# Splitting h·W1[D:] into its leading and its low part in PSUM instead of on VectorE, with other places for the row and list pieces

## The chip, the core and the metric

The kernel runs on one core of a Trainium2 chip, with TensorE (PE, and PEld for its weight loads), VectorE (DVE), ScalarE (ACT), GpSimd (POOL) and the DMA queues. The metric is the time of one execution on the device, in microseconds (us).

## The reference, cut to what matters

There are B = 16 graphs over the same N = 1024 nodes with D = 256 features, and one sparse adjacency matrix (about 0.8% of the entries and the diagonal are not zero).

```python
pre_u = einsum('bud,dk->buk', h, W1[:d])
pre_v = einsum('bvd,dk->bvk', h, W1[d:])
hidden = relu(pre_u[:, :, None, :] + pre_v[:, None, :, :] + b1)
S   = sigmoid(einsum('buvk,ko->buvo', hidden, W2)[..., 0] + b2[0])
a_t = einsum('buv,bud->bvd', S * A_a, h)
m_t = einsum('uv,bud->bvd', A_m, h) * h
z_t = beta1 * h + beta2 * (a_t @ Wa + ba) + beta3 * (m_t @ Wm + bm)
```

The kernel works on the edges alone. A *block* is 4 of the 16 graphs and 128 of the 1024 target nodes v; there are 32 blocks. A block has two windows of 64 target nodes, and a window has five chunks of 128 edges, so that a block is ten *steps*, s = 0 to 9, and the kernel has 320 steps, n = 0 to 319.

## The kernel before

For each step, 128 rows of a table in DRAM are gathered by edge (`fetch`): a row holds pre_u of four graphs and then h of four graphs. Then, in this order:

```python
def expand(n):                      # PE: pre_v, one row an edge, two steps ahead
    pcs[n] = psc.tile([P, GD], FP, name="pc")
    for h in range(2):
        nc.tensor.matmul(pcs[n][:, c], marks[n // TW][:, j * P:(j + 1) * P], cuts[k][:, w, c], start=True, stop=True)

def left_adj(n):                    # ACT: the edge's weight at the target's place
    nc.scalar.activation(lefts[n][:, :m, :, 0, :], onehot[...], AF.Copy, scale=val[:, i, j:j + 1])

def gate(n):
    nc.vector.tensor_tensor(t, fetched[n % NF][:, :GD]..., pcs.pop(n)..., ALU.add)     # DVE, 128x1024
    for b in range(GB):
        nc.vector.scalar_tensor_tensor(t[:, b, :], t[:, b, :], 0.0, w2_b, ALU.max, ALU.mult, accum_out=sc[:, b:b + 1])
    nc.scalar.activation(gt, sc, AF.Sigmoid, bias=b2_b)                                # ACT
    for b in range(GB):
        nc.scalar.activation(lefts[n][:, :m, b, 1, :], lefts[n][:, :m, b, 0, :], AF.Copy, scale=gt[:, b:b + 1])

def aggregate(n):                   # PE, a step later: sums over edges into acc
    for b in range(GB):
        nc.tensor.matmul(accs[h]..., left[:, i, b]..., f[:, GD + b * D:GD + (b + 1) * D], ...)
```

`expand` multiplies by a matrix of zeros and ones in float32r. To lose nothing, pre_v + b1 of a block is split into a leading part, rounded to float32r, and a low part. `X` holds both: for window 0 the leading parts of its 64 nodes lie in partitions 0 to 63 and the low parts in 64 to 127, and for window 1 the other way round. `halves` makes X for the next block, in two halves of 512 columns:

```python
def halves(k):
    X = cuts[k] = big.tile([P, NW, GD], FR, name="X")
    low = one.tile([P, GD], FR, name="low")
    for h in range(2):
        step = yield
        c = slice(2 * h * D, (2 * h + 2) * D)
        p = small("p")
        add_row(p, b1_p)                                  # PE: the bias
        half_product(p, hTs[order[k]], w_v, h, True)      # PE: h W1[D:]
        nc.scalar.copy(X[:, 0, c], p)                     # ACT: rounds to float32r
        after(step + 1, lambda c=c, p=p: nc.vector.tensor_tensor(
            low[:, c], p, X[:, 0, c].bitcast(FP), ALU.subtract))
    yield
    nc.scalar.copy(X[W:, 1, :], X[W:, 0, :].bitcast(FP))
    for w in range(NW):
        yield
        nc.scalar.copy(X[(1 - w) * W:(2 - w) * W, w, :], low[w * W:(w + 1) * W].bitcast(FP))
```

All tiles made by `small` are 128x512 of PSUM with the name "misc", and there are two buffers for them, taken in turn. The others that use them:

```python
def rows(k, tab=None):        # a row piece of the table: pre_u of 128 nodes, in two halves
    for h in range(2):
        step = yield
        p = small("p")
        half_product(p, hTs[k], w_u, h, False)
        nc.scalar.copy(tab[:, c], p)
    after(step + 1, lambda: nc.sync.dma_start(table[g][nt * P:(nt + 1) * P, :GD], tab))

def turn_over(k, w, q, step): # acc, copied out, is transposed into LT
    pt = small("pt")
    for i in range(4):
        nc.tensor.transpose(pt[:, i * P:(i + 1) * P], ev[:, r, c * P:(c + 1) * P], ident)
    nc.scalar.copy(LT..., pt...)
    # ... and after(step + 1): LT of A_m is multiplied by h on VectorE (times_h)

def block_end(k):             # LT times Wm and Wa, in four sends at s = 3, 4, 5, 6
    #   pz = small("pz") for each half; then after(step + 1):
    nc.vector.scalar_tensor_tensor(hb[:, 2 * h:2 * h + 2, :], hb[...], be1, pz..., ALU.mult, ALU.add)
```

`lists(vt)` makes the edge lists of 128 target nodes in about ten pieces, mostly small VectorE instructions; the lists of vt = 0 to 3 are made ahead of the steps and those of 4 to 7 among them. Each engine runs its instructions in the order in which the code emits them. The loop, cut:

```python
for n in range(total + 2):
    k, s = divmod(n, T)                       # T = 10
    aggregate(n - 1); fetch(n - 1 + NF)       # NF = 5 gather buffers
    # at s = 0, 3, 5, 8: acc is copied out (ACT, "ev")
    gate(n); left_adj(n + 1)
    if n % TW == 1: load_mark(n // TW + 1)    # ACT: a 128x640 cast, at s = 1 and 6
    do(n)                                     # what after() put here
    expand(n + 2)
    for i in advance.get(n, ()): next(made[i], None)           # list pieces
    # turn_over at s = 1 (of the block before), 7 (twice) and 9; block_end at 3 to 6
    if k + 1 < BS and s in (0, 2, 3, 4, 6): go(parts, n)       # halves of the next block
    if n in loads: load_hT(loads[n]); ...
    if n in at: go(piece, n)                                   # row pieces
```

## Time and profile before

The time is 1200.83 us, the median of three runs (1200.64 to 1201.29). The profiled execution has a span of 1195.2 us.

| group of the profile | count | mean of one | what it is |
|---|---|---|---|
| L539 DVE 128x1024 | 320 | 1215 ns | the addition of a gate |
| L543 DVE 128x256 | 1280 | 422 ns | relu, times W2, sum |
| L523 PE 128x512 | 640 | 454 ns | expand |
| L560 PE, 32 columns | 4096 records | 394 ns | aggregate, four at a time |
| L384 PE w_v and w_u | 448 records each | 384 and 390 ns | pre_v and the table rows |
| L608 PE | 992 records | 379 ns | LT times Wm and Wa |
| L612 DVE 128x512 | 62 | 744 ns | the sum into h_blk |
| L418 ACT 128x512 | 64 | 583 ns | the leading part into X |

A line of a group gives line, engine, operation, tiles (out<-in), shapes and count; then busy time in us, the mean of one in ns, and the idle time of the engine just before, with what ended it. A mean is a latency: instructions of one engine overlap at their ends, so that a series advances by less than the sum of the means. A float32 product stands as two records. A line of the time line gives start and length in us, then the same names, and in brackets the idle time of the engine before it.

### The profile page before, as it was taken

How to read it: one execution, taken by the hardware profiler on the slowest of the kernel's cores; microseconds unless marked ns; L12 is line 12 of the kernel's file. 1: busy time of each engine (PE TensorE's matmuls, PEld its weight loads, DVE VectorE, ACT ScalarE, POOL GpSimd, SP SyncE). 2: the span in 40 equal slices, each digit the busy share in tenths (PEclk: the TensorE clock that was granted, in tenths of full speed). 3: DMA queues.
4: the chain of work that ended last, by engine and by line, in shares of the span. 5: the costliest groups of instructions: out<-in, count | busy, mean ns of one | idle time of the engine just before them, and what ended most of it. 6: DMA issues, size and time to landing. Idle time of an engine off the chain costs nothing. (4 is left out here: it accounts for less than half of the span.)

```text
span 1195.2 us, 23788 instructions
## 1 busy us (share of the span) xinstructions
PE 1097.9 (92%) x7633; PEld 724.7 (61%) x7633; DVE 1066.9 (89%) x3515; ACT 840.4 (70%) x2498; POOL 426.1 (36%) x428
## 2 busy tenths in 40 slices
PE   7667988999889898999999999999999999999986
PEld 6544655666556565666666666666666666666653
DVE  8769879989988988899899999999999999999994
ACT  3346666677667665777777777787878777777873
POOL 1557652433263226333233333333333333333330
PEclk9968899999999999999999999999999999999998
DMA  9988889899979978999999999999999999999992
GB/s 279 312 307 261 258 319 333 315 336 377 320 254 373 361 244 302 357 384 360 351 329 379 359 331 371 362 356 386 358 367 345 356 324 326 326 341 328 335 340 76
DMA packets 147046, 391.39 MB, mean 327 GB/s; under 512 B 16752, under 2 KB 105328, under 8 KB 110704
## 3 DMA queue, kind: packets, MB, share of 16 engines
q0 software_dynamic: 50016, 300.50, 68.5%
q1 hardware_dynamic: 81616, 74.99, 19.6%
q10 hardware_dynamic: 15280, 14.29, 3.7%
q8 instruction: 63, 1.03, 0.3%
q14 instruction: 71, 0.58, 0.1%
HBM read 393.78 MB, written 50.33 MB: 372 GB/s over the span
## 5 line engine op out<-in xcount | busy, mean ns | idle before, releaser
L453 POOL DMA_INDIRECT fetched<-table,uidx x320 | 329.7, 1030 | 675.5 <-PE acc L560 509.6
L543 DVE SCALAR_TENSOR_TENSOR t<-t,w_b 128x256 f32<-128x256 f32 x1280 | 469.3, 422 | 20.1 <-ACT LT L581 0.5
L539 DVE TENSOR_TENSOR t<-fetched,pc 128x1024 f32<-128x1024 f32 x320 | 388.8, 1215 | 22.4 <-DMA fetched<-table,uidx 8.6
L560 PE MATMUL acc<-fetched,left 128*32 128x256 f32 x4096 | 334.2, 394 | 32.3 <-ACT left L549 16.8
L549 ACT ACTIVATE left<-left,gt 128x32 f32<-128x32 f32 (+1 forms) x1280 | 299.4, 304 | 10.4
L523 PE MATMUL pc<-X,mark 128*128 128x512 f32 x640 | 238.1, 454 | 21.1 <-DVE t L539 13.6
L560 PEld LDWEIGHTS acc<-fetched,left 128*32 128x32 f32 x4096 | 129.9, 110 | 177.2 <-issue 46.9
L546 ACT ACTIVATE gt<-sc,b_b 128x4 f32<-128x4 f32 x320 | 95.3, 298 | 140.5 <-DVE t L543 133.9
L523 PEld LDWEIGHTS pc<-X,mark 128*128 128x128 f32 x640 | 97.2, 191 | 156.6 <-issue 102.2
L608 PE MATMUL misc<-w_a,LT 128*128 128x256 f32 x496 | 127.3, 379 | 0.0
L608 PE MATMUL misc<-w_m,LT 128*128 128x256 f32 x496 | 127.1, 378 | 0.0
L384 PE MATMUL misc<-w_u,hT 128*128 128x256 f32 x448 | 109.2, 390 | 11.0 <-ACT few L298 3.6
L533 ACT ACTIVATE left<-onehot,val 128x128 f32<-128x128 bf16 (+1 forms) x320 | 116.5, 364 | 0.0
L384 PE MATMUL misc<-w_v,hT 128*128 128x256 f32 x448 | 107.9, 384 | 0.0
L543 DVE DVE_READ_ACCUMULATOR t<-t,w_b 128x1 f32 x1280 | 104.2, 81 | 0.0
L608 PEld LDWEIGHTS misc<-w_m,LT 128*128 128x128 f32 x496 | 93.7, 189 | 17.2
L384 PEld LDWEIGHTS misc<-w_u,hT 128*128 128x128 f32 x448 | 85.8, 195 | 27.3 <-issue 4.4
L608 PEld LDWEIGHTS misc<-w_a,LT 128*128 128x128 f32 x496 | 94.2, 190 | 12.8
L568 ACT COPY ev<-acc 128x512 f32<-128x512 f32 x128 | 75.1, 587 | 34.7 <-PE acc L560 26.8
L341 POOL DMA_INDIRECT val<-in_adjT_dram,vidx x80 | 83.6, 1046 | 33.4 <-issue 21.9
L384 PEld LDWEIGHTS misc<-w_v,hT 128*128 128x128 f32 x448 | 86.7, 194 | 14.3
L581 ACT COPY LT<-misc 128x512 f32<-128x512 f32 x128 | 71.1, 575 | 24.0 <-PE pc L523 12.0
(158 smaller groups left out, 830.9 us busy)
## 6 DMA issues: line engine op xcount, KB each, us to landing
h_blk<-in_x_dram SPq DMA_DIRECT2D x31, 512.0 KB
out_dram<-h_blk SPq DMA_DIRECT2D x31, 512.0 KB
hT<-in_xT_dram SPq DMA_DIRECT2D x28, 512.0 KB
table<-tab SPq DMA_DIRECT2D x26, 512.0 KB
table<-in_x_dram ACTq DMA_DIRECT2D x24, 512.0 KB
fetched<-table,uidx POOLq DMA_INDIRECT x320
table<-in_x_dram SPq DMA_DIRECT2D x8, 512.0 KB
table<-fetched SPq DMA_DIRECT2D x6, 512.0 KB
```

The source lines that it names most:

```text
L341: nc.gpsimd.indirect_dma_start(out=val[:, i, j:j + 1], out_offset=None, in_=adj_flat, in_offset=bass.IndirectOffsetOnAxis(ap=vidx[:, i, j: ...
L384: nc.tensor.matmul(p[:, bb * D:(bb + 1) * D], hT[:, 2 * h + bb, i, :], wt[:, i, :], start=(i == 0 and not begun), stop=(i == DC - 1), skip ...
L453: nc.gpsimd.indirect_dma_start(out=fetched[n % NF], out_offset=None, in_=table[g], in_offset=bass.IndirectOffsetOnAxis(ap=uidx[:, vt * NW ...
L523: nc.tensor.matmul(pcs[n][:, c], marks[n // TW][:, j * P:(j + 1) * P], cuts[k][:, w, c], start=True, stop=True)
L533: nc.scalar.activation(lefts[n][:, :m, :, 0, :], onehot[:, i, o:o + m, :].unsqueeze(2).to_broadcast([P, m, GB, V]), AF.Copy, scale=val[:, ...
L539: nc.vector.tensor_tensor(t, fetched[n % NF][:, :GD].rearrange("p (b d) -> p b d", b=GB), pcs.pop(n).rearrange("p (b d) -> p b d", b=GB), ...
L543: nc.vector.scalar_tensor_tensor(t[:, b, :], t[:, b, :], 0.0, w2_b, ALU.max, ALU.mult, accum_out=sc[:, b:b + 1])
L546: nc.scalar.activation(gt, sc, AF.Sigmoid, bias=b2_b)
L549: nc.scalar.activation(lefts[n][:, :m, b, 1, :], lefts[n][:, :m, b, 0, :], AF.Copy, scale=gt[:, b:b + 1])
L560: nc.tensor.matmul(accs[h][b * 2 * V:(b + 1) * 2 * V, r, :], left[:, i, b].rearrange("p k v -> p (k v)"), f[:, GD + b * D:GD + (b + 1) * D ...
L568: nc.scalar.copy(evs[q], accs.pop(q))
L608: nc.tensor.matmul(pz[:, bb * D:(bb + 1) * D], LTs[k][:, c, 2 * h + bb, i, :], wt[:, c, :], start=False, stop=(i == 1 and c == DC - 1), sk ...
```

## The change

The low part is no longer made by VectorE. TensorE adds minus one times the leading part to the PSUM tile that holds h W1[D:] + b1, so that the low part is what remains there, and ScalarE copies it from PSUM to its places in X. The copies are made half by half, right after that product, so `halves` needs two sends (s = 0 and 2) instead of five. The row pieces and list pieces get other places among the ten steps, some pieces ahead of the first step change their places too, and two pieces of list 3 move behind the first expansion.

```diff
+    minus = fixed([P, P], "minus", FR)
+    nc.vector.tensor_scalar(minus, ident, -1.0, None, ALU.mult)
 ...
     def halves(k):
         X = cuts[k] = big.tile([P, NW, GD], FR, name="X")
-        low = one.tile([P, GD], FR, name="low")
         for h in range(2):
 ...
             nc.scalar.copy(X[:, 0, c], p)
-            after(step + 1, lambda c=c, p=p: nc.vector.tensor_tensor(
-                low[:, c], p, X[:, 0, c].bitcast(FP), ALU.subtract))
-        yield
-        nc.scalar.copy(X[W:, 1, :], X[W:, 0, :].bitcast(FP))
-        for w in range(NW):
-            yield
-            nc.scalar.copy(X[(1 - w) * W:(2 - w) * W, w, :], low[w * W:(w + 1) * W].bitcast(FP))
+            def rest_of(c=c, p=p):
+                nc.tensor.matmul(p, minus, X[:, 0, c], start=False, stop=True, skip_group_check=True)
+                nc.scalar.copy(X[W:, 1, c], X[W:, 0, c].bitcast(FP))
+                for w in range(NW):
+                    nc.scalar.copy(X[(1 - w) * W:(2 - w) * W, w, c], p[w * W:(w + 1) * W])
+            after(step + 1, rest_of)
 ...
-    script = ("r 0 0", "r r 0", "r 1", "0 r 1 1", "0 0 r r", "1 r 0 2 2", "r r 0 0 v 2", "1 1 r r",
-              "2 r 1 r", "2 2 r r 1 1 h", "2 h 3 3", "2 2 h 3", "f h h 3", "3 3")
+    script = ("r 0 0", "r r 0", "r 1", "0 r 1 1", "0 r r 0", "1 r 0 2 2", "r r 0 0 v 2", "r r 1 1",
+              "2 1 r r", "2 r r 2 1 1 h", "2 h 3 3", "2 2 3", "f 3")
 ...
     for i, n in zip(range(EARLY, NT), (0, 20, 50, 80)):        # list pieces
-        for o in (0, 4, 5, 6, 7, 9, 11, 13, 15, 17):
+        for o in (0, 4, 6, 9, 11, 14, 16, 17, 19, 20):
 ...                                                            # (load, first half, second half) of the rows
-    plan(turn[NT:], ((0, 5, 8), (6, 12, 15), (12, 18, 22), (17, 25, 28), (24, 32, 35), (31, 38, 42), (38, 45, 48),
-                     (43, 50, 52)))
-    plan([(2, vt) for vt in range(NT)], ((62 + 10 * i, 68 + 10 * i, 73 + 10 * i) for i in range(NT)))
-    plan([(3, vt) for vt in range(NT)], ((146, 152, 157), (156, 162, 167), *((153 + 10 * i, 158 + 10 * i, 161 + 10 * i)
+    plan(turn[NT:], ((0, 7, 8), (3, 9, 11), (11, 18, 19), (15, 21, 28), (23, 29, 31), (32, 38, 39), (35, 41, 47),
+                     (42, 48, 49)))
+    plan([(2, vt) for vt in range(NT)], ((62 + 10 * i, 68 + 10 * i, 71 + 10 * i) for i in range(NT)))
+    plan([(3, vt) for vt in range(NT)], ((142, 148, 151), (152, 158, 161), *((153 + 10 * i, 158 + 10 * i, 161 + 10 * i)
                                                                              for i in range(2, NT))))
 ...
     left_adj(0)
+    for _ in range(2):
+        next(made[EARLY - 1])
 ...
-        if k + 1 < BS and s in (0, 2, 3, 4, 6):
+        if k + 1 < BS and s in (0, 2):
```

## The prediction

> **What bounds the kernel now.** I read the page's busy totals first, then the busy time by stretches, then the groups kept apart by shape, and last the time line of two blocks of ten steps. A block is found in the time line by the 128x1024 addition that opens each of its ten steps.
>
> The totals do not decide between two engines:
>
> ```profile
> PE 1097.9 (92%) x7633; PEld 724.7 (61%) x7633; DVE 1066.9 (89%) x3515; ACT 840.4 (70%) x2498; POOL 426.1 (36%) x428
> ```
>
> The stretches do. The columns are the window, its length, then busy time of PE, PEld, DVE, ACT and POOL, the clock, the DMA share and GB/s. The rows are blocks 0 to 10, 11 to 16, 18 to 23, 24 to 30, then block 21 alone and block 27 alone:
>
> ```profile
> 68.50:500.10 431.60, 387.33 (x2609) 256.15 (x2608) 379.96 (x1267) 289.42 (x860) 187.89 (x185) 0.95 0.89 311
> 500.10:700.80 200.70, 194.90 (x1371) 128.12 (x1372) 181.97 (x579) 152.98 (x460) 62.38 (x60) 0.99 0.97 359
> 733.10:927.70 194.60, 192.23 (x1389) 126.31 (x1388) 181.91 (x576) 153.26 (x462) 62.28 (x61) 1.00 0.99 361
> 927.70:1145.50 217.80, 209.73 (x1515) 133.14 (x1513) 210.83 (x672) 171.98 (x526) 71.55 (x71) 1.00 0.94 335
> 830.80:862.80 32.00, 31.43 (x229) 20.56 (x228) 30.31 (x97) 25.70 (x78) 9.72 (x10) 1.00 1.00 363
> 1021.10:1052.20 31.10, 29.96 (x218) 19.01 (x216) 30.12 (x96) 24.55 (x76) 10.20 (x11) 1.00 0.93 329
> ```
>
> Blocks 24 to 30 take 217.8 / 7 = 31.11 us each, and VectorE is busy 30.12 of block 27's 31.10: what is left is about 0.1 us between steps. They are bound by VectorE. Blocks 18 to 23, which also make table rows (two half products a block), take 32.4 on average and 32.0 at best, with both PE and VectorE near full. Blocks 0 to 10, with row pieces and lists, lose 431.6 - 380.0 = 51.6 us on VectorE.
>
> These groups carry the change (busy, then mean ns of one, then idle before):
>
> ```profile
> L419 DVE TENSOR_TENSOR low<-misc,X 128x512 fp32r<-128x512 f32 x64 | 43.9, 686 | 19.7 <-ACT X L418 19.7
> L425 ACT CAST X<-low 64x1024 fp32r<-64x1024 f32 x64 | 66.8, 1044 | 0.8
> L422 ACT CAST X<-X 64x1024 fp32r<-64x1024 f32 x32 | 33.4, 1042 | 0.4
> L581 ACT COPY LT<-misc 128x512 f32<-128x512 f32 x128 | 71.1, 575 | 24.0 <-PE pc L523 12.0 <-remote 4.8 <-PE misc L578 4.3
> ```
>
> And the places where they lie. Step 1 of block 27, ScalarE:
>
> ```profile
> 1026.75 0.30 ACT L546 ACTIVATE gt<-sc,b_b 128x4 f32<-128x4 f32 x1 [0.56 <-DVE t L543]
> 1027.08 0.96 ACT L549 ACTIVATE left<-left,gt 128x32 f32<-128x32 f32 x4
> 1027.94 0.39 ACT L533 ACTIVATE left<-onehot,val 128x128 f32<-128x128 bf16 x1
> 1028.23 0.71 ACT L516 CAST mark<-whose 128x640 fp32r<-128x640 uint8 x1
> 1028.84 0.58 ACT L581 COPY LT<-misc 128x512 f32<-128x512 f32 x1
> ```
>
> VectorE in the same block:
>
> ```profile
> 1026.63 0.69 DVE L419 TENSOR_TENSOR low<-misc,X 128x512 fp32r<-128x512 f32 x1
> 1027.23 1.21 DVE L539 TENSOR_TENSOR t<-fetched,pc 128x1024 f32<-128x1024 f32 x1
> ...
> 1029.86 0.69 DVE L591 TENSOR_TENSOR LT<-LT,hT 128x512 f32<-128x512 f32 x1
> ```
>
> Here LT, copied until 1029.42, is ready 0.44 us before VectorE multiplies it. In block 21, which makes rows, VectorE and then PE show:
>
> ```profile
> 836.32 0.68 DVE L419 TENSOR_TENSOR low<-misc,X 128x512 fp32r<-128x512 f32 x1
> ...
> 849.72 0.75 DVE L612 SCALAR_TENSOR_TENSOR h_blk<-h_blk,be,misc 128x512 f32<-128x512 f32 x1 [0.25 <-PE misc L608]
> ```
>
> ```profile
> 837.05 1.99 PE L384 MATMUL misc<-w_u,hT 128*128 128x256 f32 x8
> 838.98 1.07 PE L560 MATMUL acc<-fetched,left 128*32 128x256 f32 x16
> ```
>
> PE's row product starts at 837.05, just after the low subtraction ended at 837.00: the two PSUM buffers "misc" alternate, and the row product takes the one that held the v product. From there PE runs without a gap to the product that VectorE awaits at 849.72 (0.25 us idle), and VectorE runs without a gap to the next block's low. That is a closed loop of 31.98 us (gates at 830.78 and 862.76).
>
> **What the Trainium skill says.** "ScalarE: Activation LUTs", section "What ACT_TABLE_LOAD costs", gives 186 ns + 0.833 ns per element for an ACTIVATE with immediate operands, and an overlap of about 93 ns back to back. The trace agrees: 1,042 ns for 1,024 elements, 575 for 512, and a pair of LT copies covers 1.04 us, so the second adds about 0.47. "Perfetto Trace Analysis", section "Tensor Engine Instruction (MATMUL, LD_WEIGHTS)", says that ScalarE and VectorE are strict FIFOs; the time line shows ScalarE in program order throughout. The same page, "Optimization Strategy", says consistent bubbles can mean too few buffers; the wait of the row product on low is one. "TensorE: Matmul & The Clock Gate", "Wait — 56ns, not 53.3ns?", gives 215.7 ns start to start for 512 columns when warm; here the bias product to its follower is 1033.26 to 1033.49, 0.23, and a pc pair advances PE by 0.57.
>
> **The change, part by part.**
>
> 1. Removed from VectorE: two low subtractions a block. In block 27 a plain step is 2.81 us (1033.70 to 1036.51), and one with low 3.24 (1030.47 to 1033.70), so each is worth 0.43, not its 0.686 of latency. On VectorE alone the block would fall to 31.10 - 0.86 = 30.24.
>
> 2. Added to PE: two products with minus a block. By the pc pair each costs 0.57 / 2 = 0.28. Behind an X copy that is already done at 1026.19 and agg's end near 1026.1, it hardly waits.
>
> 3. Moved on ScalarE: three copies of 64x1024 in steps 3, 4 and 6 become six of 64x512, three in step 1 and three in step 3. The work grows by about 6 x 0.49 - 3 x 1.0, that is nothing; the place matters. In the program's order step 1 on ScalarE is now gate, left, next left, mark, three copies, LT copy. Three copies at 0.49 put the LT copy's end at 1029.42 + 1.46 = 1030.88. Without low VectorE is ready to multiply at 1029.86 - 0.43 = 1029.43. It waits 1.45, with the semaphore 1.5. Block 24 to 30: -0.43 (low in step 1) - 0.43 (in step 3) + 1.50 = +0.64 each, times 7 = +4.5 us. Later in the block nothing further is late: by step 3's copies ScalarE is some 0.2 us behind and recovers.
>
> 4. Row pieces go to steps 8 and 1 in all blocks of the middle (before, 8 and 3 up to block 16, 8 and 1 in blocks 18 to 23). In step 1 the row product takes the buffer of the v product, which is now freed by ScalarE's last copy of step 1, not by low. From gate to LT copy is 2.09 us in block 27; with three copies and the tail of the last, 2.09 + 1.46 + 0.09 = 3.6 after block 21's gate, which is at 836.43: 840.0 in place of 837.05, so PE starts 3.0 later. The rest of the loop is unchanged except for one minus product, +0.28. The loop becomes 31.98 + 3.0 + 0.28 = 35.3 us. Twelve blocks (11 to 16, 18 to 23) now take 200.7 + 194.6 = 395.3; at 35.3 they take 423.6: +28.3. Block 17, now 32.2, makes no rows in step 1: -0.4.
>
> 5. Blocks 0 to 10. The list pieces move off the steps with LT and h_blk work to 0, 4, 6, 9, and three waits of low on X (3.31, 4.42 and 2.02 us) vanish. Against that, step 1 row pieces in blocks 1 to 4 and 7 to 10 bring the loop of point 4, with the list's VectorE work inside it (about 3.6 us in a list's first block, 4.8 in its second). Block by block I get about 38 for 0, 40 for 1, 39 for 2, 40 for 3, 37 for 4, 38 for 5, 39 for 6, 35.5 for 7, 39 for 8, 40 for 9 and 35.6 for 10: 421 against 431.6, so -10. This is the softest term; the figures are estimates from the loop, the 12 us of one list's VectorE groups and the present block lengths.
>
> 6. Ahead of the first gate (68.5 us) one turn of the script goes and two list pieces move behind the first expansion: -2, an estimate.
>
> Sum: 1200.8 + 4.5 + 28.3 - 0.4 - 10 - 2 = 1221 us.
>
> **The rivals.** (a) VectorE is the bound and only its work counts: 31 blocks x 0.86 = 27 us less, about 1174. For it speaks VectorE's 97% in blocks 24 to 30; against it the order on ScalarE, where LT has only 0.44 us of slack and gets 1.46 us of copies ahead of it. (b) PE is the bound: 62 x 0.28 = 17 us more, 1218, or some 1210 with better places in the early blocks. Against it: PE in block 27 still has waits ahead of three acc groups (0.44, 0.22 and 0.48 us) that also stretch their records (1.21 for 0.64, 1.69 for 1.07 twice), some 2.9 us in all, so blocks without rows would not feel it. (c) The DMA engines are the bound, at a share of 0.97 to 0.99 in blocks 11 to 23, and 360 GB/s there; then those blocks could not get faster, and a slower loop only relieves them. VectorE's waits on fetched rows are 8.6 us in all, so this is not the leading limit. (d) The better places outweigh all: blocks 0 to 16 lose 51.6 + 18.7 us of VectorE idle; if half of it came back and the ScalarE wait were smaller than I have it, the result would be 1185 to 1195.
>
> **Range and chances.** The step-1 loop is worked from a loop that closes on the present trace within 0.1 us, so I give it +20 to +36; blocks 24 to 30 +2 to +6; the early blocks -22 to +6. Together: 1221, with 1203 to 1239 for 8 in 10. The border of 2% slower is 1224.8: slower by over 2% 0.40, within 2% 0.54, faster by over 2% 0.06.
>
> **What would show it.** Right: LT's multiplication waits about 1.5 us on ScalarE's LT copy in step 2 of blocks 24 to 30, which last 31.7; PE waits some 2.5 to 3 us ahead of the row product in step 1; blocks 18 to 23 last about 35; the first addition of h_blk in step 5 waits on PE by 2 to 3 us. Wrong: blocks 24 to 30 at 30.3 (the copies are not in the way), or 18 to 23 at 32 or less (the buffer is not what delays PE), or blocks 0 to 10 falling by over 25 us.

## The result, and the profile after

The changed kernel takes 1303.28 us (median of 4 runs, 1296.60 to 1307.78) where the kernel before takes 1200.74 (1200.37 to 1201.29): a ratio of 1.0849, 95% interval 1.0801 to 1.0897. It is slower by 8.5%. The profiled execution has a span of 1302.6 us, 107.4 more than before.

First the totals. PE's line and VectorE's (DVE) are to be held against those of before: VectorE has 33 us less work, PE 43 us more busy time, and neither is near its limit any more (PE 88% and VectorE 79% of the span, from 92% and 89%). When every engine fills a smaller share of a longer span, no engine's work has become the bound; the time lies in waits.

```profile
PE 1141.1 (88%) x7697; PEld 741.8 (57%) x7697; DVE 1033.8 (79%) x3452; ACT 861.2 (66%) x2594; POOL 430.3 (33%) x428
```

Then the stretches, in the order of before: blocks 0 to 10, 11 to 16, 18 to 23, 24 to 30, then block 21 and block 27 alone. The columns are window, length, busy time of PE, PEld, DVE, ACT, POOL, then the granted clock of TensorE (1.00 is full speed), the DMA share and GB/s.

```profile
64.30:536.90 472.60, 403.73 (x2631) 261.94 (x2632) 367.43 (x1245) 296.90 (x894) 191.50 (x188) 0.90 0.84 289
536.90:762.40 225.50, 204.03 (x1401) 131.52 (x1399) 175.94 (x568) 157.42 (x480) 61.93 (x61) 0.95 0.91 321
795.40:1024.80 229.40, 205.01 (x1402) 133.72 (x1402) 175.67 (x564) 157.36 (x480) 62.19 (x61) 0.94 0.87 308
1024.80:1254.20 229.40, 214.82 (x1529) 135.08 (x1527) 204.69 (x659) 176.86 (x547) 74.59 (x71) 1.00 0.89 317
910.10:947.40 37.30, 34.01 (x235) 22.45 (x233) 29.30 (x95) 26.39 (x81) 10.31 (x10) 0.95 0.89 313
1124.00:1156.40 32.40, 30.59 (x221) 19.26 (x218) 29.26 (x94) 25.27 (x79) 10.81 (x11) 1.00 0.89 312
```

Two things are to be seen. VectorE lost in block 27 what was taken from it (30.12 to 29.26, the 0.86 of the prediction), and the block grew all the same. And the clock, which was 0.99 and 1.00 in the blocks that make rows, is 0.95 and 0.94 there now, but 1.00 in blocks 24 to 30, which make none.

The ledger of the 107.4 us, from these windows and those of before:

| stretch | predicted | measured |
|---|---|---|
| up to the first gate | -2 | 64.3 - 68.5 = -4.2 |
| blocks 0 to 10 | -10 | 472.6 - 431.6 = +41 |
| blocks 11 to 16 and 18 to 23 | +28.3 | 454.9 - 395.3 = +59.6 |
| block 17 | -0.4 | 33.0 - 32.3 = +0.7 |
| blocks 24 to 30 | +4.5 | 229.4 - 217.8 = +11.6 |
| block 31 and the end | 0 | 48.4 - 49.7 = -1.3 |

Next the groups of instructions kept apart by shape (count, then busy, mean ns, idle before and what ended it):

```profile
L426 ACT CAST X<-misc 64x512 fp32r<-64x512 f32 x128 | 74.2, 580 | 3.3 <-PE acc L561 0.6
L424 ACT CAST X<-X 64x512 fp32r<-64x512 f32 x64 | 39.4, 615 | 0.8
L592 DVE TENSOR_TENSOR LT<-LT,hT 128x512 f32<-128x512 f32 x55 | 37.9, 689 | 71.2 <-ACT LT L582 71.2
L386 PE MATMUL misc<-w_u,hT 128*128 128x256 f32 x448 | 135.9, 460 | 63.5 <-ACT X L426 60.5 <-ACT LT L582 1.6 <-ACT tab L402 1.4
```

The last two lines name the waits: VectorE stood 71 us ahead of LT's multiplication, for ScalarE's LT copy, and PE stood 60 us ahead of row products, for the last of the three X copies. The last line has a second message: its mean is 460 ns, where it was 390 before and the same form with w_v still has 385. These records alone are 27 of PE's 43 us more (135.9 from 109.2).

The time line of block 27 shows the first wait as it arises. ScalarE, step 1:

```profile
1131.17 0.71 ACT L517 CAST mark<-whose 128x640 fp32r<-128x640 uint8 x1
1131.89 0.62 ACT L424 CAST X<-X 64x512 fp32r<-64x512 f32 x1
1132.54 1.17 ACT L426 CAST X<-misc 64x512 fp32r<-64x512 f32 x2
1133.73 0.59 ACT L582 COPY LT<-misc 128x512 f32<-128x512 f32 x1
```

And VectorE, at the end of the same step:

```profile
1134.35 0.69 DVE L592 TENSOR_TENSOR LT<-LT,hT 128x512 f32<-128x512 f32 x1 [1.81 <-ACT LT L582]
```

The mark cast and the LT copy, which stood one behind the other before, now have three copies between them. These take 1133.73 - 1131.89 = 1.84 us, and VectorE waits 1.81.

The time line of block 21 shows the second wait. PE:

```profile
915.28 0.50 PE L423 MATMUL misc<-X,minus 128*128 128x512 f32 x1
915.62 0.62 PE L524 MATMUL pc<-X,mark 128*128 128x512 f32 x2
916.08 0.60 PE L579 MATMUL misc<-ident,ev 128*128 128x128 f32 x4
919.86 3.56 PE L386 MATMUL misc<-w_u,hT 128*128 128x256 f32 x8 [3.18 <-ACT X L426]
```

The same stretch cut in three, at the start and the end of the row product:

```profile
916.60:919.80 3.20, 0.08 (x1) 0.00 (x0) 1.93 (x9) 3.15 (x8) 0.01 (x1) 0.98 0.97 361
919.80:923.40 3.60, 3.54 (x12) 2.58 (x16) 2.92 (x9) 0.59 (x2) 0.00 (x0) 0.55 0.42 162
923.40:926.60 3.20, 3.20 (x27) 2.32 (x27) 1.82 (x6) 2.13 (x7) 0.99 (x1) 1.00 0.58 164
```

While PE stands, the clock reads 0.98. During the product it is 0.55, and the eight records, 1.99 us before, take 3.56. Behind it the clock is full again. So a wait of 3.18 us cost 1.57 more after it had ended. Beside LT's 1.81, which this block has too, VectorE pays for it in the additions of two gates and in that of h_blk:

```profile
925.12 1.22 DVE L540 TENSOR_TENSOR t<-fetched,pc 128x1024 f32<-128x1024 f32 x1 [1.34 <-PE pc L524]
928.98 1.22 DVE L540 TENSOR_TENSOR t<-fetched,pc 128x1024 f32<-128x1024 f32 x1 [1.13 <-PE pc L524]
934.32 0.75 DVE L613 SCALAR_TENSOR_TENSOR h_blk<-h_blk,be,misc 128x512 f32<-128x512 f32 x1 [2.55 <-PE misc L609]
```

### The profile page after: what moved, and what is told of

The parts are those of the page before. It is cut to its first block, busy times and chain, and to the rows that moved or that the text cites. A ratio compares the mean times of both kernels' runs of the same rounds, so it can differ in the third digit from the quotient of the medians.

```text
span 1302.6 us, 24051 instructions
## 1 busy us (share of the span) xinstructions
PE 1141.1 (88%) x7697; PEld 741.8 (57%) x7697; DVE 1033.8 (79%) x3452; ACT 861.2 (66%) x2594; POOL 430.3 (33%) x428
## 5 line engine op out<-in xcount | busy, mean ns | idle before, releaser
L455 POOL DMA_INDIRECT fetched<-table,uidx x320 | 333.4, 1042 | 777.6 <-PE acc L561 634.9
L561 PE MATMUL acc<-fetched,left 128*32 128x256 f32 x4096 | 327.9, 403 | 18.8 <-ACT left L550 15.2
L524 PE MATMUL pc<-X,mark 128*128 128x512 f32 x640 | 232.3, 445 | 9.1 <-DVE t L540 9.1
L561 PEld LDWEIGHTS acc<-fetched,left 128*32 128x32 f32 x4096 | 121.0, 112 | 169.7 <-issue 61.6
L386 PE MATMUL misc<-w_u,hT 128*128 128x256 f32 x448 | 135.9, 460 | 63.5 <-ACT X L426 60.5
L524 PEld LDWEIGHTS pc<-X,mark 128*128 128x128 f32 x640 | 102.5, 192 | 124.8 <-issue 71.4
L386 PEld LDWEIGHTS misc<-w_u,hT 128*128 128x128 f32 x448 | 100.2, 230 | 86.4 <-ACT X L426 64.5
L579 PE MATMUL misc<-ident,ev 128*128 128x128 f32 x512 | 75.7, 279 | 26.8 <-ACT X L426 13.5
L592 DVE TENSOR_TENSOR LT<-LT,hT 128x512 f32<-128x512 f32 (+1 forms) x57 | 38.8, 680 | 75.1 <-ACT LT L582 75.1
L343 POOL DMA_INDIRECT val<-in_adjT_dram,vidx x80 | 84.1, 1051 | 33.0 <-issue 22.2
```

Of the source, the lines that this page charges most:

```text
L343: nc.gpsimd.indirect_dma_start(out=val[:, i, j:j + 1], out_offset=None, in_=adj_flat, in_offset=bass.IndirectOffsetOnAxis(ap=vidx[:, i, j: ...
L386: nc.tensor.matmul(p[:, bb * D:(bb + 1) * D], hT[:, 2 * h + bb, i, :], wt[:, i, :], start=(i == 0 and not begun), stop=(i == DC - 1), skip ...
L455: nc.gpsimd.indirect_dma_start(out=fetched[n % NF], out_offset=None, in_=table[g], in_offset=bass.IndirectOffsetOnAxis(ap=uidx[:, vt * NW ...
L561: nc.tensor.matmul(accs[h][b * 2 * V:(b + 1) * 2 * V, r, :], left[:, i, b].rearrange("p k v -> p (k v)"), f[:, GD + b * D:GD + (b + 1) * D ...
```

## The experiments

The kernel before took 1182.7 to 1184.8 us beside them, and 1198.3 beside e15 and e16, so each time is read as a ratio to the kernel before on the same chip and occasion. The table has the ratio with its interval, and the length of the groups of blocks in each profile; b0 and a0 are the kernel before and the changed one, unedited.

| run | ratio | 0-10 | 11-16 | 18-23 | 24-30 |
|---|---|---|---|---|---|
| b0_before | - | 414.6 | 198.4 | 197.2 | 218.9 |
| a0_after | 1.0919 (1.0869 to 1.0970) | 458.0 | 226.5 | 228.7 | 228.0 |
| e1_math_only | 1.0634 (1.0586 to 1.0682) | 443.5 | 216.2 | 225.9 | 228.6 |
| e2_places_only | 1.0034 (1.0015 to 1.0052) | 427.0 | 195.5 | 196.1 | 218.8 |
| e3_copies_behind_LT | 1.0485 (1.0446 to 1.0524) | 440.2 | 210.9 | 217.1 | 226.1 |
| e4_fill_wait | 1.0669 (1.0619 to 1.0719) | 455.9 | 215.3 | 218.7 | 229.3 |
| e5_rows_step6 | 1.0419 (1.0372 to 1.0467) | 436.3 | 204.5 | 209.5 | 229.4 |
| e8_no_minus | 1.0876 (1.0823 to 1.0928) | 461.6 | 223.3 | 226.3 | 228.7 |
| e7_hybrid | 1.0105 (1.0063 to 1.0148) | 411.4 | 203.1 | 194.5 | 225.2 |
| e9_early_halves | 1.0950 (1.0907 to 1.0992) | 435.4 | 225.6 | 229.1 | 252.1 |
| e10_early_halves_16 | 1.1222 (1.1145 to 1.1299) | 458.1 | 237.6 | 219.3 | 250.1 |
| e11_early_halves_dve | 1.0164 (1.0117 to 1.0211) | 430.3 | 199.4 | 199.9 | 221.1 |
| e12_one_copy | 1.0413 (1.0382 to 1.0444) | 438.8 | 215.6 | 212.2 | 218.5 |
| e13_both | 1.0298 (1.0268 to 1.0327) | 430.1 | 203.3 | 206.5 | 226.6 |
| e14_hybrid2 | 1.0003 (0.9985 to 1.0021) | 415.3 | 197.5 | 198.7 | 214.6 |
| e15_hybrid3 | 0.9951 (0.9929 to 0.9973) | 432.6 | 202.0 | 196.5 | 214.5 |
| e16_hybrid4 | 0.9911 (0.9877 to 0.9944) | 427.9 | 201.8 | 197.7 | 214.0 |
| e17_hybrid4_again | 0.9963 (0.9944 to 0.9983) | 413.4 | 202.6 | 198.5 | 214.4 |

The groups are those of one execution. Those of 0 to 10 differ between occasions: one program has 415.3 as e14 and 432.6 as e15, beside 1182.7 and 1198.3 of the kernel before. They are compared only where the kernel before is within 1182 and 1185. A ratio near 1 differs between occasions too, by some 0.005. That the chip is the reason is not shown: e15 and e16 ran on the chip of the same number as e1 to e8, where the kernel before had taken 1183.3 and 1184.1.

**The arithmetic alone, and the places alone (e1, e2).** e1 has the product with minus and the three copies, in the places of before. e2 has VectorE's subtraction in the places of the change.

```diff
 e1:  halves(k) as changed; script, advance, plan as before
 e2:  halves(k) and its five sends as before; script (but for those sends), advance, plan as changed
```

> The minus product and the six ScalarE copies, with the places of row and list pieces, the script and the loop of before. Theory (the copies on ScalarE hold back LT and the PSUM buffer, whatever the places): most of the loss comes with the arithmetic alone, 1270 to 1310 us; blocks 24 to 30 at 32.4 each as in the changed kernel, blocks 18 to 23 at 37 to 39. Rival (the new places of the row pieces are what costs): about 1200 to 1215, with blocks 24 to 30 at about 31 to 32 and 18 to 23 near 33.

> VectorE makes low as before (three copies of 64x1024 in steps 3, 4 and 6), with the new places of row and list pieces. Theory: the places by themselves are no loss and perhaps a small gain, 1180 to 1203 us; blocks 11 to 16 at 32 to 32.7. Rival (places are the cause): 1260 or more, with PE waits ahead of the row product in step 1.

Most of the loss is the arithmetic's: 1.0634 alone, where the places alone have 1.0034. (e1's 1260.9 us lies below the 1270 to 1310 expected, beside a kernel before that takes 17 us less here than in the pair above; its blocks, 37.7 us each in 18 to 23 and 32.7 in 24 to 30, are about those expected.) In blocks 18 to 30 e1 has nearly the whole loss of a0. In blocks 11 to 16 the places are worth 3 us by themselves (195.5 against 198.4 in b0) and cost 10 with the arithmetic (226.5 in a0 against 216.2 in e1), because they move a row product from step 3 to step 1, behind the copies.

In blocks 0 to 10 the places cost 12 us (427.0 against 414.6), the arithmetic 29, and both together 43 (a0), so that there the two costs nearly add. The places' part lies in blocks 1, 3, 6 and 9, each the second of a list: 45.9, 43.9, 39.4 and 42.0 us in e2 where b0 has 40.6, 37.9, 36.3 and 38.9, while the other blocks together are 5 us shorter. VectorE's low, which waited for X in step 1 of other blocks before, waits 4.1, 4.2 and 2.3 us for it in step 3 of blocks 1, 3 and 9, and LT waits 2.0 to 2.8 in their step 8. Block 3 of e2:

```profile
205.66 0.69 DVE L420 TENSOR_TENSOR low<-misc,X 128x512 fp32r<-128x512 f32 x1 [4.20 <-ACT X L419]
...
227.84 0.69 DVE L591 TENSOR_TENSOR LT<-LT,hT 128x512 f32<-128x512 f32 x1 [2.77 <-ACT LT L581]
```

**The copies behind LT (e3).** The three copies stay in step 1 and 3, but are issued on ScalarE after the LT copy.

```diff
-                nc.scalar.copy(X[W:, 1, c], X[W:, 0, c].bitcast(FP))       # in rest_of
-                for w in range(NW): nc.scalar.copy(..., p[w * W:(w + 1) * W])
+                late_copies.append((X, c, p))
 ...
+        copy_late()                       # behind turn_over, ahead of the list pieces
```

> The changed kernel with the three copies emitted behind the LT copy of step 1 (and the list piece of the step behind them). Theory: VectorE's wait of 1.81 us for LT in step 2 goes, so that blocks 24 to 30 fall from 32.4 to 30.6, but the row product of step 1 waits some 0.6 us longer for the buffer, so blocks with rows stay at 37 to 38.5: 1285 to 1305 in all. Rival (the LT wait is what costs in the blocks with rows too): 1260 to 1270, every block 1.8 us shorter.

LT's wait in step 2 is gone in block 21, and the row product there waits for the LT copy in place of the X copies. It starts before the copies out of PSUM are made, so the tile it takes is now the other one:

```profile
864.28 0.57 ACT L591 COPY LT<-misc 128x512 f32<-128x512 f32 x1
...
864.91 2.51 PE L386 MATMUL misc<-w_u,hT 128*128 128x256 f32 x8 [2.27 <-ACT LT L591]
```

It won half of the loss back (1.0485 against the 1.0919 of a0), more than the theory had, because the row product's wait became shorter where a longer one was expected: row blocks took 35.2 us on average up to block 16 and 36.2 in 18 to 23. In blocks 24 to 30 the theory missed to the other side: 30.6 each was expected and 32.3 measured, 2 us of the loss of 9 in all, because the first addition of h_blk in step 5 then waits 1.1 to 1.4 us for PE.

**The wait filled (e4).** The wait of the row product is left as it is, but ten redundant products of the pc pair are put ahead of it, whose result is written again over itself. PE has more work, and in block 21 the wait of 3.2 us becomes one of 0.9.

```diff
+            if s == 1 and k:
+                for _ in range(5):
+                    again_expand(n + 2)          # the pair of products of expand once more
```

> The changed kernel with five pairs of redundant expand products (written again to the same tile) ahead of each row product of step 1, about 2.9 us of PE work in a wait of 3.2. Theory (the wait lets the granted clock fall to about half, and the eight records of the row product then take 3.5 us and not 1.9): the clock stays at 1.0, the row product takes 1.9, blocks 11 to 16 and 18 to 23 fall from about 37.3 to 35.6, total 1265 to 1285 although PE does more. Rival (the row product is slow for its own reasons, or PE's work is the bound): 1303 or more.

Block 21 of e4, PE's time line, and the clock in the stretch of the row product:

```profile
885.81 2.54 PE L534 MATMUL pc<-X,mark 128*128 128x512 f32 x10
889.24 1.99 PE L386 MATMUL misc<-w_u,hT 128*128 128x256 f32 x8 [0.89 <-ACT X L426]
```

```profile
889.20:891.20 2.00, 1.96 (x12) 1.48 (x14) 1.37 (x2) 0.59 (x1) 0.00 (x0) 1.00 0.55 229
```

The product starts as late as before, for the same releaser, and takes 1.99 us at a clock of 1.00. Work added to PE made the kernel faster by 2.3% (1.0669 against 1.0919); the twelve row blocks fell by 11.2 + 10.0 = 21 us, or 1.8 each. In all twelve the row product takes 1.99 to 2.00 us, behind waits of 0.85 to 2.14, where in a0 it takes 3.27 on average: 1.28 of the 1.8. So the slow product is the clock's doing, and the clock's fall the wait's. The other 0.5 this run does not explain.

The size of the wait that brings this about isn't sharp. In the row blocks of the changed kernel (11 to 16 and 18 to 23) waits of 3.2 to 4.5 us were followed by a product of 2.7 to 3.8 us in eleven blocks and by one of 1.99 in the twelfth (block 20); in those of e3 waits of 1.8 were followed by 1.99 each time, but of five between 2.2 and 2.6 two were followed by 1.99 and three by 2.5, 3.3 and 3.5. In e12 two products were slow behind 1.83 and 1.84 (blocks 8 and 11), and others behind 1.8 were not. "TensorE: Matmul & The Clock Gate" of the Trainium skill, Part 1, section "What's actually happening", says that the clock goes to 4/8 after at least one idle window of about 3.4 us. The half agrees with the 0.55 here; the runs show the fall also behind shorter waits.

**Row pieces elsewhere (e5).** The row pieces of step 1 go to step 6.

```diff
-    plan([(2, vt) for vt in range(NT)], ((62 + 10 * i, 68 + 10 * i, 71 + 10 * i) for i in range(NT)))
+    plan([(2, vt) for vt in range(NT)], ((62 + 10 * i, 68 + 10 * i, 76 + 10 * i) for i in range(NT)))
     # and so in the other two lists
```

> The changed kernel with each row piece of step 1 moved to step 6 (the others stay; the last at step 1). Theory (in blocks with rows the loss is the wait of step 1's row product for the buffer that ScalarE copies from, and the clock that falls in it): blocks 11 to 16 and 18 to 23 fall from about 37.5 to 33 to 34.5, the granted clock there stays at 1.0, ratio to before 1.03 to 1.045. Rival (PE's added work is what costs in blocks with rows): they stay above 36, ratio 1.075 or more.

Row blocks fell from 38 to 34.1 us on average up to block 16 and 34.9 in 18 to 23, and the ratio to 1.0419. LT's wait of 1.82 in step 2 stays, one of 1.1 to 1.4 in step 8 is added; blocks 24 to 30, without rows, are what they were (229.4).

**Both (e13).** The edits of e3 and of e5 together.

> The changed kernel with two edits together: the three copies come behind the LT copy on ScalarE, and the row pieces of step 1 move to step 6. Theory (two separate waits, LT's on the copies and the row product's on the PSUM tile): the gains add, row blocks take 33 to 34 us, blocks 24 to 30 about 32 each, and the ratio to the kernel before is 1.015 to 1.035. Rival (one and the same wait seen twice): no better than the better of the two alone, 1.04 or more.

The ratio, 1.0298, is in the range of the theory, and the row blocks took 33.9 us on average up to block 16 and 34.4 in 18 to 23, the latter a little above the 33 to 34 expected. But the gains do not add. In blocks 11 to 16 e3 won 15.6 us over a0, e5 22.0 and both together 23.2; in blocks 18 to 23 it is 11.6, 19.2 and 22.2. Once the row product has left step 1, taking LT's wait of 1.82 us away is worth 0.2 to 0.5 us a block, because VectorE then waits elsewhere. Block 21 of e5, and then of e13:

```profile
852.22 0.69 DVE L592 TENSOR_TENSOR LT<-LT,hT 128x512 f32<-128x512 f32 x1 [1.82 <-ACT LT L582]
...
872.22 0.69 DVE L592 TENSOR_TENSOR LT<-LT,hT 128x512 f32<-128x512 f32 x1 [1.34 <-ACT LT L582]
```

```profile
850.72 0.75 DVE L622 SCALAR_TENSOR_TENSOR h_blk<-h_blk,be,misc 128x512 f32<-128x512 f32 x1 [1.42 <-PE misc L618]
...
861.79 0.69 DVE L601 TENSOR_TENSOR LT<-LT,hT 128x512 f32<-128x512 f32 x1 [1.37 <-ACT LT L591]
```

So LT's wait and the row product's have one cause, the copies, but they are not two costs to be added up. What of e3's own gain in row blocks (2.6 and 1.9 us each) is LT's and what is the row product's, which waits less there too, no run tells apart.

**The product left out (e8).** The subtraction is left out: the product with minus isn't sent, and the low part is then the whole sum once more. All copies stay.

```diff
-                nc.tensor.matmul(p, minus, X[:, 0, c], start=False, stop=True, skip_group_check=True)
```

> The changed kernel without the 62 products with minus, so that what is copied as the low part is the whole sum (this leaves out the subtraction). Theory: only 0.3 us a loop goes, ratio to before 1.075 to 1.082 where the whole change has 1.085. Rival (the PE product is the cost): 1.05 or less.

1.0876 against 1.0919, with intervals that overlap; the 1.075 to 1.082 expected had been reckoned from 1.085. The product itself is nearly free; the loss lies with the copies.

**One copy in place of three (e12).** ScalarE takes the low part out of PSUM in one 128x512 copy and spreads it later from SBUF, in steps 3, 4 and 6, as before.

```diff
-                nc.scalar.copy(X[W:, 1, c], X[W:, 0, c].bitcast(FP))
-                for w in range(NW):
-                    nc.scalar.copy(X[(1 - w) * W:(2 - w) * W, w, c], p[w * W:(w + 1) * W])
+                nc.scalar.copy(low[:, c], p)
 ...                                        # and the three copies of 64x1024 in three later sends
```

> The changed kernel with its product and its places, but ScalarE takes the low part out of PSUM in one 128x512 copy (about 0.58 us) in steps 1 and 3, and spreads it from SBUF in steps 3, 4 and 6 as the kernel before does. Theory (the loss is the time for which three ScalarE copies stand ahead of the LT copy and hold the PSUM tile): the LT wait in step 2 of blocks 24 to 30 falls from 1.8 to 0.5 to 0.8 us, the row product of step 1 waits about 2 us in place of 3.2 and its clock stays at 1.00, row blocks take 34 to 35 us in place of 37.3, and the ratio to the kernel before is 1.03 to 1.05. Rival (what costs is that ScalarE, of whatever size its copy, and PE stand in this chain at all): row blocks at 36.5 or more and a ratio of 1.075 or more.

Block 21 of e12, the lines of ScalarE, PE and VectorE about the LT copy:

```profile
864.52 0.57 ACT L425 CAST low<-misc 128x512 fp32r<-128x512 f32 x1
865.00 0.58 ACT L586 COPY LT<-misc 128x512 f32<-128x512 f32 x1
...
865.15 1.99 PE L386 MATMUL misc<-w_u,hT 128*128 128x256 f32 x8 [1.83 <-ACT low L425]
865.61 0.69 DVE L596 TENSOR_TENSOR LT<-LT,hT 128x512 f32<-128x512 f32 x1 [0.33 <-ACT LT L586]
```

The copy is followed by LT's after 0.48 us, where the three took 1.84. LT waits 0.33 (less than the 0.5 to 0.8 expected), the row product 1.83, at full clock; block 21 lasts 34.3 and the ratio is 1.0413. Blocks 24 to 30 are back at the length of b0 (218.5 against 218.9). In the row blocks, 35.9 us on average up to block 16 and 35.4 in 18 to 23, it did less than expected: there the product is still slow in five of twelve, behind waits of 1.84 to 3.11. The time for which the copies stand ahead of LT and hold the tile is thus a little over half of the loss (9.2% fell to 4.1%). Of the rest the trace of block 21 shows a part: ScalarE, with its gate, left and mark ahead, comes to this copy 1.8 us after PE wants the tile.

**The halves earlier (e9, e10, e11).** Here the two halves are sent a block earlier, in steps 8 and 9, so that the copies meet other steps; row pieces are in steps 1 and 2 (e9) or 6 and 1 (e10). e11 has the places of e9 but VectorE's subtraction.

```diff
-        if k + 1 < BS and s in (0, 2, 3, 4, 6):
+        if n in (0, 2, 3, 4, 6) and k == 0 or k + 2 < BS + (s < 8) and s in SENDS and n >= 8:
```

> The minus product and its copies as in the change, but the two half products of X are made a block earlier, in steps 8 and 9 (their copies in 9 and 0), row pieces in steps 1 and 2, lists as before. Theory (VectorE's saving is real, but it needs a place where ScalarE's copies precede nothing urgent, and PE's work spread over the block): no wait for LT in step 2, blocks 25 to 30 at 30.2 to 30.8 where before has 31.1, blocks 18 to 23 at 32 to 33, ratio 0.97 to 0.995. Rival (the arithmetic costs wherever it stands): blocks 25 to 30 at 31.5 or more, ratio 1.01 or more.

> As the run before, with row pieces in steps 6 and 1 instead of 1 and 2. Theory: the same in blocks 25 to 30 (no rows there); blocks 18 to 23 within 1 us a block of that one, either way. Rival as there.

> The places of the second run of this call, but VectorE subtracts as before (in steps 9 and 0; copies in 0, 3 and 4). Theory: VectorE bounds it again, blocks 25 to 30 at 31.0 to 31.2, slower than with the minus product by 0.5 to 0.9 us a block there; ratio 0.985 to 1.005. Rival (places alone make any gain): equal to the run with the minus product, within 0.2 us a block.

All three expectations failed: 1.0950, 1.1222 and 1.0164. In e9 the row product starts after 0.41 us at full clock, but LT waits about 3 us in step 2 of nearly every block, and in blocks 19 to 21, 25 and 26 PE's product for the bias waits 2.4 to 2.8 for the X copies; blocks 24 to 30 rose to 36 us. Block 25 of e9:

```profile
1043.15 0.69 DVE L592 TENSOR_TENSOR LT<-LT,hT 128x512 f32<-128x512 f32 x1 [2.99 <-ACT LT L582]
```

With VectorE's subtraction the same places lose far less (e11, blocks 24 to 30 at 31.6 us each), though they too are no gain. The three copies cost in each of the places tried, and moving them in one piece only chose who waits.

**The new arithmetic only where no row is made (e7, e14).** Both are the kernel before up to block 23, but for the row places of the change in blocks 7 to 16, which e14's expectation leaves out. From block 24 e7 has the product with minus, three copies behind LT, the mark cast in steps 2 and 6 and the first addition of h_blk a step later. e14 has the product with the one copy of e12, the same mark cast, both additions of h_blk a step later and one of the two `turn_over` of step 7 in step 8 (the edit of e14):

```diff
+        by_pe = k > 24
 ...
+                if by_pe:
+                    nc.tensor.matmul(p, minus, X[:, 0, c], start=False, stop=True, skip_group_check=True)
+                    nc.scalar.copy(low[:, c], p)
+                else:
+                    nc.vector.tensor_tensor(low[:, c], p, X[:, 0, c].bitcast(FP), ALU.subtract)
 ...
-            after(step + 1, add)
+            after(step + (2 if 24 <= k < BS - 2 else 1), add)
 ...
-        if n % TW == 1 and n // TW + 1 < total // TW:
+        if n % T in ((2, 6) if n >= 240 else (1, 6)) and n // TW + 1 < total // TW:
 ...
         if s == 7 and k < BS:
             turn_over(k, 0, 0, n)
+        if s == (8 if 24 < k < BS - 1 else 7) and k < BS:
             turn_over(k, 0, 1, n)
```

> Before's arithmetic, with table rows 2 and 3 at the new places, up to block 23; from block 24 on, where no rows are made, the minus product with its copies behind the LT copy of step 1, mark's cast moved from step 1 to 2, and the first addition of h_blk from step 5 to 6. Theory (VectorE's work is worth its time only where ScalarE and PE leave room): blocks 25 to 30 at 30.2 to 30.6 where before has 31.1, blocks 11 to 16 at 32.2, ratio to before 0.985 to 0.996. Rival (some other wait takes its place): blocks 25 to 30 at 31 or more, ratio 0.997 to 1.005.

> The kernel before up to block 23; from block 24 on, where no row is made, the product with minus and one ScalarE copy of the low part, the mark at step 2, and the additions of h_blk one step later, in steps 6 and 8. Theory (VectorE's saving of 0.86 us a block shows where neither LT nor h_blk waits on what was added): blocks 25 to 30 take 30.3 to 30.8 us in place of 31.1, and the ratio to the kernel before is 0.99 to 1.00. Rival (PE's chain from its wait in step 1 on takes VectorE's place as the limit): blocks 25 to 30 at 31.1 or more and a ratio of 1.005 or more.

e7 missed its expectation (1.0105): blocks 25 to 30 lasted 32 us, with a wait of 1.2 us for PE ahead of an addition of h_blk in step 7. In e14 blocks 26 to 30 last 30.4 to 30.5, and no wait of over 0.15 us is left on VectorE there. Block 27 alone:

```profile
1009.00:1039.50 30.50, 30.29 (x222) 19.52 (x219) 29.19 (x95) 25.28 (x78) 10.90 (x11) 1.00 0.93 333
```

VectorE is busy 29.19 of 30.50, and PE in nearly all of it. Blocks 26 to 30 average 30.43 us, 0.68 less than the 31.11 of before, of the 0.86 taken from VectorE. Which of e14's four edits beside the product brings this, no run tells apart. The whole stood at 1.0003, above what 4 us out of 1183 would make of it. In the profile the first gate comes at 73.1 us where b0 has 70.6, and block 23 lasts 36.2, with a late start and the clock at 0.80 behind it; why, no run shows.

**The same again, and with the prelude of the change (e15, e16, e17).** e15 is the program of e14 once more, on another chip; its expectation counts the row places of blocks 11 to 16 in. e16 adds the order of the change ahead of the first gate, and e17 is e16 again, on a third chip.

```diff
 e16, e17, against e14:
     left_adj(0)
+    for _ in range(2):
+        next(made[EARLY - 1])
-              "2 r 1 r", "2 2 r r 1 1 h", "2 h 3 3", "2 2 h 3", "f h h 3", "3 3")
+              "2 1 r r", "2 r r 2 1 1 h", "2 h 3 3", "2 2 h 3", "f h h 3")
 ...                       # and two entries of the script's line above as changed
```

> The kernel before up to block 23 but for one place (the first row piece of blocks 11 to 16 in step 1 in place of 3, as the change has it), and from block 24 on the product with minus, one ScalarE copy, the mark at step 2 and the additions of h_blk in steps 6 and 8. Theory (the row place of the change is worth 2 to 3 us over blocks 11 to 16 where VectorE makes low, and the saving on VectorE 4 us over blocks 24 to 30): blocks 11 to 16 at 195 to 196 us, 24 to 30 at 213 to 215, ratio to the kernel before 0.994 to 0.998. Rival (both are given back in other blocks, as what is gained there starts transfers that others wait for): ratio 0.999 or more.

> The kernel of e15 with the change's order of the prelude as well (its script, and two list pieces behind the first expansions). Theory (the first gate then comes 3 to 5 us earlier, and the first blocks keep their length): ratio 0.990 to 0.995. Rival (what the prelude gains the list pieces give back in blocks 0 and 1): the first gate earlier, blocks 0 and 1 together longer by as much, ratio within 0.002 of that of e15.

> The kernel of e16, unedited, on whatever chip it meets. One and the same program, run as e14 and as e15, gave ratios of 1.0003 and 0.9951, so that a ratio near 1 depends on the chip by some 0.005, more than the intervals of each. Theory (the earlier first gate, 5 us, and the shorter blocks 24 to 30, 4 us, are the kernel's own): ratio 0.988 to 0.996, first gate 65 to 68 us, blocks 24 to 30 at 213.5 to 215. Rival (the 0.9911 of e16 was mostly its chip): 0.997 or more.

e16's order beats both kernels, by less than 1%: 0.9911 on one chip and 0.9963 (0.9944 to 0.9983) on another (e17). The latter lies between the 0.996 of e17's theory and the 0.997 of its rival, so that e17 does not decide between the two. For e14's order the two occasions disagree (1.0003 and 0.9951). The first gate comes at 66.3 us in e16 where e15, on the same chip, has 71.3, and blocks 0 and 1 last 88.4 us in e16, 88.2 in e15: the prelude's gain is kept. The stretch of blocks 24 to 30 in e16:

```profile
925.10:1139.00 213.90, 211.65 (x1529) 135.92 (x1527) 204.03 (x658) 177.70 (x541) 74.19 (x71) 1.00 0.94 337
```

PE now fills 211.65 of 213.90: there, by its busy time, it is the bound. Blocks 11 to 16 missed (202.0 in e15, where 195 to 196 was expected), for block 11 alone: it lasts 38.4 us in e15, 38.8 in e16 and e17 and 39.7 in e7, but 34.0 in e14, which is the program of e15; blocks 12 to 16 last 32.0 to 34.4 in e15 to e17. PE's line at its start in e16 shows why:

```profile
495.69 3.75 PE L386 MATMUL misc<-w_u,hT 128*128 128x256 f32 x8 [4.72 <-DMA hT<-in_xT_dram]
```

A load of hT for the row piece came late, and here too the product behind a long wait takes nearly twice its time. An earlier load was not tried; against the 32 us of the blocks behind it, it would be worth some 6 us, an estimate.

## Why the prediction was wrong

Right were the direction and, in blocks 11 to 30, the waits, what ends them and where they stand. In the profiled pair the sum is short by 87 us: the parts foretold 20.4, and 107.4 were measured. The step that failed by most is the fifth, which took blocks 0 to 10 for a gain (51 us); the fourth had "the rest of the loop is unchanged", where the clock fell (31 us, of them 14 in the row products and 8 in longer waits); the third mis-sized the copies (7 us). By its own parts:

1. *Removed from VectorE, 0.43 a subtraction.* Right. In block 27 the two steps with low went from 3.32 and 3.24 us to 2.89 and 2.81.

2. *Added to PE, 0.28 a product.* A little more, 0.34 (915.28 to 915.62), and of little weight: without it the ratio is 1.0876 in place of 1.0919 (e8).

3. *Three copies at 0.49, a wait of 1.5, blocks 24 to 30 at 31.7.* The wait is there in every block, in step 2, as said. The mis-sized term is the copy: three took 1.84 us in place of 1.46, so 0.61 each. The 0.49 came from a pair of LT copies, which overlap. In block 26 of the changed kernel such a pair still takes 1.07 us for two of 0.58:

```profile
1118.86 1.07 ACT L582 COPY LT<-misc 128x512 f32<-128x512 f32 x2
```

"ScalarE: Activation LUTs" of the Trainium skill, section "What ACT_TABLE_LOAD costs", has an overlap of about 93 ns back to back; here the first copy lasts 0.62 and the next starts 0.65 after it, with none. Its formula, which the prediction found to agree with the trace, does so for 1,024 elements, but gives an estimate of 613 ns for 512, where the LT copies take 575. That the three write one tile, X, is not the reason, for the pair writes one tile too. What the copies into X have of their own is that they cover 64 partitions: in the changed kernel none of the 250 neighbours on ScalarE of which one is a copy of 64 partitions overlap, not even the mark cast, which writes another tile, with the first copy (1131.17 + 0.71 = 1131.88, then 1131.89), where before the LT copy started 0.10 ahead of the end of that cast. Why that is so, no run shows. The 0.38 of difference makes the predicted 1.45 into 1.83, and 1.81 was measured. The other part of the miss (229.4 / 7 = 32.8 us a block, against 32.4 in block 27) is mostly waits of 0.2 to 1.0 us for gathered rows at the start of four of the blocks.

4. *The loop of the row product, 31.98 + 3.0 + 0.28 = 35.3.* The wait is there, on the releaser named, and PE started 4.07 us after ScalarE's gate (915.79 to 919.86) where 3.6 was said, for the same copies. What failed is "the rest of the loop is unchanged": a wait of over 3 us halves PE's clock for the next product, and in block 21 this adds 1.57. With 3.45 in place of 3.0 the loop closes to 0.1: 31.98 + 3.45 + 0.34 + 1.57 = 37.34, and block 21 lasts 37.24. Over the twelve blocks the row products take 3.18 us on average in place of 1.99, which is 14 of the 31 us that were missing, and PE waits 3.65 ahead of them on average in place of 3.0, another 8. The waits are longest (4.2 to 4.5) in blocks 15, 18, 19 and 23, whose second gate waits 1.1 to 1.9 us for gathered rows. Some 8 us stay open. e4 shows the clock's part, e3 and e5 the wait's.

5. *Blocks 0 to 10, -10.* This is the step that failed by most, 51 us, and in sign. It took the better places for a gain and the loop for the only cost. e2 shows that the places alone lose 12 us in these blocks: the waits of low on X that were to vanish came back in step 3 of the lists' second blocks. e1 shows that the arithmetic alone costs 29 there without any new place. The copies hold more than a row product here: in blocks 1 to 4 of the changed kernel PE waits 2.5 to 4.1 us in step 2 for them, in two of the four ahead of the transposes for LT, and LT waits 1.8 to 3.3. PE and VectorE in block 1:

```profile
124.99 1.11 PE L579 MATMUL misc<-ident,ev 128*128 128x128 f32 x4 [4.05 <-ACT X L426]
```

```profile
127.13 0.69 DVE L592 TENSOR_TENSOR LT<-LT,hT 128x512 f32<-128x512 f32 x1 [3.32 <-ACT LT L582]
```

I had called the term the softest and yet given it a range of only -22 to +6. In block 0 of the profiled pair LT waited 7.3 us in step 8, behind a wait of PE that nothing in the profile explains; in a0 the block is 6 us shorter. This part stays open, and no run sums up the 51 us wait by wait.

6. *The prelude, -2.* It was -4.2. e16 has its first gate 5 us earlier than e15 and does not give this back in the next blocks.

Of the rivals, (a) fell: VectorE's work is less by 33 us, where it had 27, and the kernel did not get shorter. (b) is not what happened, since the product is nearly free, but PE's busy time (30.29 of 30.50 us in block 27 of e14) speaks for it in blocks 24 to 30 of e14 and e16, once the waits are gone. (c) the DMA share fell with the longer blocks; no run speaks for it. (d) had the early blocks as a gain, and e2 speaks against that. Whether a third buffer for misc would end the row product's wait was not tried.

## What to carry to other kernels

Work taken from a busy engine pays only if what replaces it does not stand ahead of something that is waited for on its new engine, or hold a buffer longer: ask when the tile comes free, not only how long the instruction takes. When a predicted wait leaves TensorE without work for 2 us and more, reckon with a slow clock on what follows (it came behind most such waits here, not behind all), and look at the mean of the group behind the wait. Take the time of a copy in a row from copies of its own shape, partitions included. And two waits with one cause are not added up: try what is left of one when the other is gone.

## What the runs showed of the hardware that I had not expected

- TensorE's granted clock fell to 0.55 for the 3.6 us behind a wait of 3.18, in the midst of a kernel that keeps it busy for 88% of the time. With ten redundant products ahead of each such row product it stayed at 1.00 in block 21, and the kernel was 2.3% faster (e4).
- Copies of 64 partitions on ScalarE did not overlap with the instruction ahead or behind, whatever its tile (none of 250 such neighbours in the changed kernel): those of 64x512 followed each other by 0.61 us on average (0.58 to 0.62 long). A copy of 128x512 started 0.10 before the end of the mark cast and let the LT copy follow after 0.48 (e12). Three copies of half the partitions cost 1.84, nearly four times the one copy of all.
